# Mixture of experts behind cross-attention: first tiles of experts 4 to 7 from five items, narrower two-group tiles, and a later load of the last items' inputs

## The chip, the cores and the metric

The kernel runs on one core of a Trainium2 chip. The metric is the device time of one execution in microseconds; the median of the runs of the kernel before is 442.06.

## The reference, cut to what matters

Eight items (batch elements) of 256 tokens with 256 features go through a cross-attention block and then through a feed-forward layer with eight experts, of which each token uses two.

```python
x = x + xattn(layernorm(x), ctx, ctx, mask, gamma, beta)   # ctx: 8 x 77 x 256; softmax over 77; layernorm of the result
h = layernorm(x)                                           # 2048 tokens
p = softmax(h @ w_gate)                                    # 8 experts; keep the two largest, divide by their sum
gu = einsum('bsd,edh->ebsh', h, w_gate_up)                 # per expert 256 x 2048
act = silu(g) * u                                          # g, u: the halves of gu, 1024 each
x = x + sum over experts of p_e * (act_e @ w_down_e)       # per expert 1024 x 256
```

The kernel computes an expert only for the tokens that chose it. There are 4096 token-expert pairs.

## The kernel before, in words

**The two kinds of work.** A *unit* (`unit(b)`, L445) is one item: its attention, its normalised row, its choice of two experts, and the place of each token in the list of its expert. It ends with two stores: the item's x to the output (L826, SyncE's queue) and its normalised rows with gate values to a scratch tensor `xn_rows` (L860, ScalarE's queue; item 1's on SyncE's). A *tile* (`tile_work(t)`, L1214) takes rows of one expert: GpSimd gathers them from `xn_rows` (L1195) by a list of indices; TensorE transposes them (L1278); ScalarE copies them (L1285); TensorE forms g and u (L1335), ScalarE silu (L1357), VectorE the product (L1364), TensorE the down product (L1396, or L1393 in turned form); VectorE multiplies by the gate (L1445), and GpSimd adds the rows to the output by a scattering DMA (L1199). VectorE computes the gate of a tile (L1292) from the gathered rows.

**The tiles.** Tiles 0 to 7 are the *first tiles* of experts 0 to 7, up to 128 rows each. They can start before all items are routed: `PARTS` says after how many items which experts' first tiles are filled, `(2, 0, 1)`: expert 0 after two items, `(3, 1, E)`: experts 1 to 7 after three. For each entry `first_table(i)` (L922) takes the lists as they stand: a product on TensorE picks the tokens (L934), VectorE writes the indices (L947) and clears those experts in the lists (L951), a second product gives the counts (L938), and an expert with fewer than 128 tokens begins to count anew (L957 to L966). The counting of the next item waits for that. After item 7, `second_table` (L976) divides what is left into tiles: thirteen *narrow* tiles of 128 rows, and eight *wide* ones of two groups, one per expert, of 128 rows and of `WIDE[k]` rows. The experts are sorted by their remainder, and the k-th gets the k-th width. Where a remainder exceeds its width, it takes another narrow tile; more than thirteen of those would go through a slow path (`rest_tile`). A wide tile costs its whole width W = 128 + `WIDE[k]`, filled or not; with `WIDE[k]` below 100 the down product is turned, so that it too costs W columns. `ORDER1` sets the order of narrow and wide tiles.

**The order.** Every operation is recorded by `add(engine, cost, emit, needs, rank, lag, ...)`; `Order.run` then simulates the engines with these costs and lags and writes out an order for each engine, where among operations that can begin at nearly the same time the lowest rank goes first. On the chip each engine follows its order and waits for what an instruction needs. Units rank before tiles on TensorE, so the units' pieces stand between the tiles' groups of eight matmuls. Matmuls on constant data (`fill`, L327) keep TensorE busy until tile 0 begins.

**The loads.** Expert weights are 1 MB each for the two halves of gate-up (L264) and for down (L265); three sets of buffers (lanes) hold them, tile t of the first eight using lane t mod 3. SyncE issues them in the planner's order. At the start the inputs of items 0 to 5 (`UE = UA + 3`, `UA` the number of items of the last entry of `PARTS`, 3) and the weights of tile 0 and gate-up of tile 1 are issued. What is left, `load_late` (L257), has the down matrix of tile 1 and x and mask of items 6 and 7; it waits for one-element memsets on VectorE (L1313 to L1315) that need tile 0's gate, which holds it back until item 1's store and tile 0's gather are through. Tile 2's weights are held back in the same way until the gate of tile 1.

Of the kernel before, what the change touches and what calls it, by code (L numbers as in the profile page):

```python
# [33 lines left out]
class Order:  # L34
# [18 lines left out]
    def add(self, eng, cost, emit=None, needs=(), rank=0.0, lag=None, takes=(), uses=(), after=(), slack=0.0):  # L53
        lag = self.LAG[eng] if lag is None else lag
        w = Work(eng, cost, emit, list(needs), list(after), rank, lag, list(takes), slack)
        for b in list(takes) + list(uses):
            b.users.append(w)
        self.all.append(w)
        return w
# [61 lines left out]
def kernel(  # L121
# [36 lines left out]
    nc = tc.nc  # L158
    P = 128
    B, S, D = x.shape  # L160
    T = ctx_in.shape[1]
    E = w_gate.shape[1]
# [7 lines left out]
    NL = N // P  # L170
    LANES = 3

    PARTS = [(2, 0, 1), (3, 1, E)]
    UF, UA = PARTS[0][0], PARTS[-1][0]
    UE = UA + 3
    MT0 = E

    WIDE = [128, 120, 104, 96, 80, 64, 48, 24]
    assert len(WIDE) == E and E * NL == P


# [54 lines left out]
    wd = [keep.tile([P, NF, D], F32, name=f"wd{l}") for l in range(LANES)]  # L236

    def load(what, dst, src, b0, b1, per):
        what.dma_start(dst[:, b0 * per : b1 * per, :], src[:, b0 * per : b1 * per, :])
# [14 lines left out]
    load(nc.sync, x_all, x_t, UA, UE, NT)  # L254
    load(nc.sync, m_all, mask_t, UA, UE, NT)

    def load_late():  # L257
        nc.sync.dma_start(wd[1], w_down[1].rearrange("(c p) d -> p c d", p=P))
        load(nc.sync, x_all, x_t, UE, B, NT)
        load(nc.sync, m_all, mask_t, UE, B, NT)  # L260

    def weight_dmas(l, gu, d, **kw):
        for up in range(2):
            nc.sync.dma_start(wgu[l][:, :, ts(up, F)], gu[:, :, ts(up, F)], **kw)  # L264
        nc.sync.dma_start(wd[l], d, **kw)  # L265

    def load_expert(l, e):
        weight_dmas(
            l,
            w_gate_up[e].rearrange("(c p) f -> p c f", p=P),  # L270
            w_down[e].rearrange("(c p) d -> p c d", p=P),
        )
# [23 lines left out]
    def iota(dst, pattern, base, mult):  # L296
        nc.gpsimd.iota(
            dst, pattern=pattern, base=base, channel_multiplier=mult, allow_small_or_imprecise_dtypes=True
        )
# [31 lines left out]
    add = order.add  # L331
# [19 lines left out]


    c_in = [add("in", 0.0, lag=3.8 if b == 0 else 7.3 if b < UA else 14.0) for b in range(B)]
    late = add("sp", 1.0, load_late, [], -1999.0, lag=5.0)
    x_in = [add("in", 0.0, lag=(4.2, 7.0, 10.0)[b] if b < UA else 17.0) if b < UE else late for b in range(B)]
    m_in_ = [add("in", 0.0, lag=4.3 if b == 0 else 11.6 if b < UA else 18.6) if b < UE else late for b in range(B)]
    wg_in = add("in", 0.0, lag=4.6)
# [78 lines left out]

    anew = [const.tile([P, E], BF16, name=f"anew{i}") for i in range(len(PARTS))]
    ahead = list(before)
    for i, (units, _, _) in enumerate(PARTS):
        ahead[units * NT] = anew[i]  # L440
# [460 lines left out]
    def table_constants():  # L901
# [12 lines left out]
        for k in range(E):  # L914
            nc.gpsimd.memset(widths[:, k : k + 1], float(WIDE[k]))
        iota(bases, [[NL, E]], 0, 0)
# [5 lines left out]
    def first_table(i):  # L922

        units, e0, e1 = PARTS[i]
        last = routed[units - 1]
# [237 lines left out]

    snaps = [first_table(i) for i in range(len(PARTS))]
    table = [None, second_table([p[1] for p in snaps])]


    def weights_of(at, m):
        e = nc.sync.value_load(at[0:1, m : m + 1], min_val=0, max_val=E - 1)
        return (  # L1170
            w_gate_up[bass.ds(e, 1)].rearrange("o (c p) f -> p (o c) f", p=P),
            w_down[bass.ds(e, 1)].rearrange("o (c p) d -> p (o c) d", p=P),
        )

    def load_weights(t):
        f, m, l = tiles[t]
        if f == 0:
            return load_expert(l, m)
        kw = {}
        if f == 1:  # L1180
            kw = dict(cond=nc.sync.value_load(new[0:1, m : m + 1], min_val=0, max_val=1), cond_hint=False)
        weight_dmas(l, *weights_of(eid_w if f == 2 else eid, m), **kw)

    def part_of(t):
        return next(i for i, (_, e0, e1) in enumerate(PARTS) if e0 <= tiles[t][1] < e1)

# [24 lines left out]
    def known(w):  # L1211
        return [] if w is None else [w]

    def tile_work(t):  # L1214
# [4 lines left out]
        if wide:  # L1219
            n = WIDE[m]  # L1220
            groups = [(P, idx[1][:, MT1 + m : MT1 + m + 1]), (n, idx[1][:n, MT1 + E + m : MT1 + E + m + 1])]
# [11 lines left out]
        r, rp = -1000.0 + t, 1.0e6 + 100.0 * t  # L1233
# [7 lines left out]
        if t < LANES - 1:  # L1241
            weights = add("in", 0.0, lag=(24.0, 33.0)[t])
        elif f == 0:
            needs += [w for s in stored[:UF] for w in s] if t < LANES else []
            if t == LANES - 1:

                needs.append(
                    add("dve", 0.08, lambda: nc.vector.memset(wgu[l][:1, 0, :1], 0.0), [held_back["gc"]], r)
                )
            weights = add("sp", 2.0, lambda: load_weights(t), needs, r, lag=8.0)  # L1250
        else:
            weights = add("sp", 1.0, lambda: load_weights(t), needs, r, lag=8.0 if wide else 3.0)

        b_x, got, where = [], [], []
        for n, at in groups:
# [3 lines left out]
            def gather(n=n, at=at, dst=where[-1]):  # L1259
                pool_rows(t, at, dst[:n], in_=xn_d)  # L1260
                if t == MB - 1:
# [5 lines left out]
                    lag=3.0, takes=[b_x[-1]], after=gathers[-1:],  # L1267
# [19 lines left out]
        def gate(i):  # L1287
            n, src = groups[i][0], where[i]
            gs = hpool.tile([P, 2], F32, tag="gs", name=f"gs{t}_{i}", bufs=4)
            v["gc", i] = hpool.tile([P, 1], F32, tag="gc", name=f"gc{t}_{i}", bufs=4)  # L1290
            mine = float(m) if f == 0 else em_w[:n, m : m + 1] if wide else em[:n, L1 + m : L1 + m + 1]
            nc.vector.scalar_tensor_tensor(  # L1292
                gs[:n], src[:n, EXP : EXP + 2], mine, src[:n, GATE : GATE + 2],
                ALU.is_equal, ALU.mult, accum_out=v["gc", i][:n],
            )
# [5 lines left out]
        if t == 0:  # L1301
            held_back["ex"].after.append(xT)
            add("pe", 0.0, lambda: fills.update(stop=True), [tp], rp - 129, lag=0.0)
        gc = [
            add("dve", 0.25, lambda i=i: gate(i), [got[i]] + known(et), r, takes=[b_gs[i]], uses=[b_x[i]])
            for i in range(len(groups))
        ]


        if t == 0:  # L1310

            late.needs += [
                add("dve", 0.08, lambda: nc.vector.memset(wd[1][:1, 0, :1], 0.0), gc, r),  # L1313
                add("dve", 0.08, lambda: nc.vector.memset(x_all[:1, UE * NT, :1], 0.0), gc, r),
                add("dve", 0.08, lambda: nc.vector.memset(m_all[:1, UE * NT, :1], 0), gc, r),  # L1315
            ]
# [206 lines left out]
    for t in range(MB):  # L1523
        if t == MT0:
            guessed = add(
                "sp", 3.0, lambda: load_expert(TURN1[0], HELD[0]), [lane_last[TURN1[0]]], -1000, lag=3.0
            )
        tile_work(t)
# [40 lines left out]
```

## Time and profile before

| | |
|---|---|
| median of three runs | 442.06 us (441.53 to 445.3) |
| profiled execution | 441.23 us, span 439.5 us |
| TensorE busy | 426.5 us (97%) |
| VectorE, ScalarE, GpSimd busy | 151.8, 121.7, 132.2 us |
| two thirds of TensorE's time | g and u, 268.0 us in 1856 matmuls |
| down products | 127.0 us in 592 matmuls |
| read and written by DMA | 102.69 MB and 8.71 MB |

How to read the rows: a line of a timeline has the start, the length, the engine, the line of the kernel, the operation, output and inputs by the program's names, shapes and the number of instructions; in brackets stands the idle time ahead of it and what ended it. A matmul's row lasts longer than its turn, since matmuls overlap: eight g of 128 columns follow one another in 0.89 us though each row lasts 0.28. A row of windows has the window, its length, the busy times of TensorE, its weight loads, VectorE, ScalarE and GpSimd with instruction counts, the granted clock of TensorE, the share of the DMA engines and GB/s.

### The profile page before, as it was taken

What the parts mean: (1) busy time and instruction counts of PE and PEld (TensorE: products, weight loads), DVE (VectorE), ACT (ScalarE), POOL (GpSimd) and SP (SyncE); (2) the same over time, 40 slices, a digit from 0 to 9 for tenths busy, and PEclk for the clock granted to TensorE, in tenths of its full rate; (3) what the DMA queues carried; (4) which work ended last, traced back from release to release, by engine and by line L of the source; (5) the groups of instructions that cost most, each with busy time, mean ns of one, the idle gap of its engine ahead of it and who ended that gap; (6) DMA issues with size and microseconds to landing.
All of it is one profiled execution on the core that took longest, in us unless ns stands there. A gap on an engine that the chain in (4) does not pass through costs nothing. (4 is left out here: it accounts for less than half of the span.)

```text
span 439.5 us, 8064 instructions
## 1 busy us (share of the span) xinstructions
PE 426.5 (97%) x2961; PEld 398.8 (91%) x2961; DVE 151.8 (35%) x682; ACT 121.7 (28%) x298; POOL 132.2 (30%) x155
## 2 busy tenths in 40 slices
PE   8998899999999999999999999999999999999995
PEld 6877789899999998999999999999999999999994
DVE  4897268766772122111111221112121112212111
ACT  6785466863311111011111111111111111221110
POOL 7642552432216230332033202321413304212121
PEclk9999889999999999999999999999999999999999
DMA  6995598999998994883289945376428257781011
GB/s 157 335 354 151 170 388 260 328 303 316 322 322 255 383 326 110 283 269 81 88 239 304 319 168 157 95 248 209 115 41 297 32 188 228 230 279 17 9 18 34
DMA packets 54563, 92.58 MB, mean 211 GB/s; under 512 B 5544, under 2 KB 41124, under 8 KB 54513
## 3 DMA queue, kind: packets, MB, share of 16 engines
q1 hardware_dynamic: 45388, 81.25, 54.7%
q0 software_dynamic: 6688, 8.59, 10.2%
q10 hardware_dynamic: 2437, 2.11, 1.5%
q8 instruction: 26, 0.43, 0.4%
q14 instruction: 24, 0.20, 0.1%
HBM read 102.69 MB, written 8.71 MB: 253 GB/s over the span
## 5 line engine op out<-in xcount | busy, mean ns | idle before, releaser
L1335 PE MATMUL g<-xgT,wgu 128*128 128x128 f32 (+8 forms) x928 | 134.1, 294 | 0.5 <-ACT xgT L1285 0.5
L1335 PE MATMUL u<-xgT,wgu 128*128 128x128 f32 (+8 forms) x928 | 133.9, 294 | 0.0
L1335 PEld LDWEIGHTS g<-xgT,wgu 128*128 128x128 f32 x928 | 123.1, 191 | 2.4 <-ACT xgT L1285 0.7
L1335 PEld LDWEIGHTS u<-xgT,wgu 128*128 128x128 f32 x928 | 123.4, 191 | 1.6
L1364 DVE TENSOR_TENSOR hT<-sil,u 128x512 f32<-128x512 f32 (+7 forms) x74 | 47.9, 648 | 167.2 <-PE u L1335 162.2
L1199 POOL DMA_INDIRECT out_dram<-y,idx x37 | 57.5, 1554 | 148.5 <-DVE gs L1292 78.3
L1396 PE MATMUL o<-wd,hT 128*128 128x256 f32 (+2 forms) x432 | 100.4, 385 | 0.0
L1396 PEld LDWEIGHTS o<-wd,hT 128*128 128x128 f32 (+2 forms) x432 | 81.1, 193 | 10.9
L1357 ACT ACTIVATE sil<-g 128x512 f32<-128x512 f32 (+7 forms) x74 | 41.8, 565 | 149.4 <-PE g L1335 143.1
L1195 POOL DMA_INDIRECT xg<-xn_rows,idx x37 | 39.0, 1055 | 109.1 <-PE tp L1278 88.0
L1285 ACT COPY xgT<-tp 128x256 f32<-128x256 f32 (+8 forms) x29 | 11.9, 411 | 102.9 <-PE tp L1278 102.5
L1445 DVE TENSOR_SCALAR y<-o,gc 128x256 f32<-128x256 f32 (+2 forms) x26 | 12.6, 484 | 54.0 <-PE o L1396 54.0
L1393 PE MATMUL o<-hT,wd 128*128 128x224 f32 (+4 forms) x160 | 26.6, 324 | 0.0
L1393 PEld LDWEIGHTS o<-hT,wd 128*128 128x128 f32 x160 | 25.9, 190 | 0.0
L327 PE MATMUL filled<-filler 128*128 128x256 bf16 x114 | 17.1, 289 | 1.3 <-DVE cT L396 1.3
L1278 PE MATMUL tp<-ident,xg 128*128 128x128 f32 (+7 forms) x74 | 12.8, 269 | 2.6 <-DMA xg<-xn_rows,idx 2.6
L1278 PEld LDWEIGHTS tp<-ident,xg 128*128 128x128 f32 (+7 forms) x74 | 9.7, 141 | 5.9 <-DMA xg<-xn_rows,idx 3.1
L1445 DVE TENSOR_SCALAR y<-rows,gc 128x256 f32<-128x256 f32 (+5 forms) x10 | 4.3, 476 | 28.4 <-PE rows L1425 28.4
L327 PEld LDWEIGHTS <-filler 128*128 128x128 bf16 x114 | 11.1, 104 | 3.0 <-DVE cT L396 1.3
L833 POOL TENSOR_TENSOR rx<-ss,neg_half 128x2 f32<-128x2 f32 x8 | 5.7, 707 | 19.7 <-DVE ss L830 19.3
L1413 ACT COPY oT<-o 128x224 f32<-128x224 f32 (+4 forms) x10 | 3.2, 318 | 28.2 <-PE o L1393 28.2
L645 PE MATMUL v<-av_w,pT 77*128 77x256 f32 x32 | 9.6, 426 | 0.8 <-ACT xT L522 0.8
(207 smaller groups left out, 306.2 us busy)
## 6 DMA issues: line engine op xcount, KB each, us to landing
wgu<-in_L_ffn_w_gate_up_dram SPq DMA_DIRECT2D x60, 1024.0 KB
wd<-in_L_ffn_w_down_dram SPq DMA_DIRECT2D x30, 1024.0 KB
out_dram<-x_all SPq DMA_DIRECT2D x8, 256.0 KB
xn_rows<-xnr ACTq DMA_DIRECT2D x7, 260.0 KB
x_all<-in_x_dram SPq DMA_DIRECT2D x3, 256.0 KB
x_all<-in_x_dram SPq DMA_DIRECT2D x1, 768.0 KB
xg<-xn_rows,idx POOLq DMA_INDIRECT x37
out_dram<-y,idx POOLq DMA_INDIRECT x37
```

The costliest lines, as they stand in the source:

```text
L327: nc.tensor.matmul(filled, filler[:, :P], filler, start=True, stop=True)
L645: nc.tensor.matmul(v["v"][:, j, :], v["pT"][:, j, :], av_w[:, b, KC:], start=True, stop=True)
L1195: nc.gpsimd.indirect_dma_start(out=tile_, out_offset=None, in_=in_[:n], in_offset=at, bounds_check=n - 1, oob_is_err=False)
L1199: nc.gpsimd.indirect_dma_start(out=out_[:n], out_offset=at, in_=tile_, in_offset=None, bounds_check=n - 1, oob_is_err=False, **kw)
L1278: nc.tensor.transpose(v["tp"][:, c, off : off + n], src[:n, ts(c, P)], ident[:n, :n])
L1285: nc.scalar.copy(v["xT"][:, :, :W], v["tp"][:, :, :W])
L1335: nc.tensor.matmul(v[tag, h][:, i, : W if wide else P], wgu[l][:, c, bass.ds(off + (h + i) * P, P)], v["xT"][:, c, : W if wide else P], st ...
L1357: nc.scalar.activation(v["sil", h], v["g", h][:, :, : min(W, per)], AF.Silu)
L1364: nc.vector.tensor_tensor(v["hT", h // held][:, bass.ds(h % held, FG), : min(W, per)], v["sil", h], v["u", h][:, :, : min(W, per)], ALU.mult,)
L1393: nc.tensor.matmul(v["o", d][:, :W], wd[l][:, i, ts(d, P)], hT[:, :W], **kw)
L1396: nc.tensor.matmul(v["o", d][:n], hT[:, offs[d] : offs[d] + n], wd[l][:, i, :], **kw)
L1445: nc.vector.tensor_scalar(v["y", i][:n], src, gc, None, ALU.mult)
```

## The change

`PARTS` gets a third entry: experts 1 to 3 are filled from three items, experts 4 to 7 from five, so there is a third first table, after item 4, and tiles 4 to 7 gather only after item 4's rows are stored. `UA` stays 3. Five of the eight widths of the wide tiles fall. The late load is split: the down matrix of tile 1 is loaded as before, held by tile 0's gate (`load_down`); x and mask of items 6 and 7 come after tile 2's weights in SyncE's order (`late.after`), held by tile 1's gate, and the planner gets another rank and lag for them.

```diff
-    PARTS = [(2, 0, 1), (3, 1, E)]
-    UF, UA = PARTS[0][0], PARTS[-1][0]
+    PARTS = [(2, 0, 1), (3, 1, 4), (5, 4, E)]
+    UF, UA = PARTS[0][0], PARTS[1][0]
...
-    WIDE = [128, 120, 104, 96, 80, 64, 48, 24]
+    WIDE = [128, 120, 104, 88, 72, 48, 40, 16]
...
+    def load_down():
+        nc.sync.dma_start(wd[1], w_down[1].rearrange("(c p) d -> p c d", p=P))
+
     def load_late():
-        nc.sync.dma_start(wd[1], w_down[1].rearrange("(c p) d -> p c d", p=P))
         load(nc.sync, x_all, x_t, UE, B, NT)
         load(nc.sync, m_all, mask_t, UE, B, NT)
...
-    late = add("sp", 1.0, load_late, [], -1999.0, lag=5.0)
+    late = add("sp", 1.0, load_late, [], -997.9, lag=11.0)
...
             weights = add("sp", 2.0, lambda: load_weights(t), needs, r, lag=8.0)
+            if t == LANES - 1:
+                late.after.append(weights)
...
         if t == 0:
-
+            hold = add("dve", 0.08, lambda: nc.vector.memset(wd[1][:1, 0, :1], 0.0), gc, r)
+            add("sp", 0.5, load_down, [hold], r, lag=3.0)
+        if t == LANES - 2:
             late.needs += [
-                add("dve", 0.08, lambda: nc.vector.memset(wd[1][:1, 0, :1], 0.0), gc, r),
                 add("dve", 0.08, lambda: nc.vector.memset(x_all[:1, UE * NT, :1], 0.0), gc, r),
                 add("dve", 0.08, lambda: nc.vector.memset(m_all[:1, UE * NT, :1], 0), gc, r),
             ]
```

## The prediction

> **What bounds the kernel now.** I read the page first. Its parts 1 and 2:
>
> ```profile
> span 439.5 us, 8064 instructions
> PE 426.5 (97%) x2961; PEld 398.8 (91%) x2961; DVE 151.8 (35%) x682; ACT 121.7 (28%) x298; POOL 132.2 (30%) x155
> PE   8998899999999999999999999999999999999995
> PEclk9999889999999999999999999999999999999999
> ```
>
> TensorE is the bound: from 60 us to its last matmul it is full, except for 0.85 us near 81. So a change counts only if it shortens TensorE's stream, or opens or closes a hole in it. The holes lie before 60 us, and there the clock row shows an 8 twice. So the next view is TensorE's timeline there:
>
> ```profile
> 48.01 1.02 PE L528 MATMUL lps<-cT,xT 128*128 128x86 f32 x8
> 50.52 0.44 PE L1278 MATMUL tp<-ident,xg 128*128 128x128 f32 x2 [1.49 <-DMA xg<-xn_rows,idx]
> 50.79 1.03 PE L1396 MATMUL o<-wd,hT 128*128 128x256 f32 x4
> 52.44 1.12 PE L640 MATMUL gkp<-av_w,pT 77*128 77x85 f32 x4 [0.62 <-DVE xw L605]
> 53.36 1.98 PE L645 MATMUL v<-av_w,pT 77*128 77x256 f32 x4
> 55.13 4.60 PE L1396 MATMUL o<-wd,hT 128*128 128x256 f32 x12
> ```
>
> and the same stretch in windows of 2 us, where the granted clock (third from the right) halves at 52 us:
>
> ```profile
> 50.00:52.00 2.00, 1.30 (x6) 0.85 (x6) 0.43 (x7) 0.37 (x1) 1.48 (x2) 1.00 0.36 83
> 52.00:54.00 2.00, 1.56 (x6) 1.50 (x7) 0.56 (x3) 1.20 (x4) 1.86 (x3) 0.51 0.78 246
> 58.00:60.00 2.00, 2.00 (x10) 1.66 (x10) 1.68 (x13) 1.40 (x6) 0.48 (x1) 0.78 1.04 377
> ```
>
> Tile 1's gathered rows come 1.49 us late. Who held them: GpSimd's timeline, ScalarE's queue, and the DMA queues from 44 to 46 us (q10 is ScalarE's, q1 SyncE's; packets, MB, share).
>
> ```profile
> 40.41 0.40 ACTq L860 DMA_DIRECT2D xn_rows<-xnr  x1
> 47.52 1.09 POOL L1195 DMA_INDIRECT xg<-xn_rows,idx  x1 [9.59 <-DMA xn_rows<-xnr]
> ...
> q1 hardware_dynamic: 380, 0.32, 98.6%
> q10 hardware_dynamic: 36, 0.04, 11.2%
> ...
> q10 hardware_dynamic: 222, 0.22, 63.0%
> q1 hardware_dynamic: 354, 0.12, 46.3%
> ```
>
> Item 2's rows, issued at 40.4 to 40.8, move only from 44.5 to 46.1, and the gather starts 1.4 us later. In front stand the three transfers of the late load: one 1.05 MB down matrix, 0.52 MB of x, 0.16 MB of mask.
>
> **The change, part by part.** *Narrower tiles.* The cost is read from whole tiles: W=224 takes 287.27 to 305.43 (18.16 us), W=208 takes 317.24 to 334.12 (16.88), W=176 takes 14.32, W=152 takes 12.40. The slope is 0.080 us a column. The five changed widths lose 8+8+16+8+8 = 48 columns: -3.84 us, all on TensorE and hidden by nothing. All five were below the limit of 100 for the turned product, so the form stays. The routing of the given inputs fits: after five items every expert holds at least 128 rows, the sorted remainders are 114, 90, 73, 45, 19, 18, 15, 10, nothing spills and 13 narrow tiles suffice. With the old split the remainders 89, 73 would spill.
>
> *The late load.* The down matrix stays where it was; x and mask of items 6 and 7 go behind tile 2's weights on SyncE's queue. Item 2's store then has 0.68 MB less ahead, at 0.35 MB/us 1.9 us. The gather starts near 45.6 and lands 3.0 us later (47.52 to 50.5), 48.6, against 49.0 when TensorE gets there: the hole falls from 1.49 to about 0.2, -1.3. In the new order v of item 3 precedes gkp; gkp still waits for the xw of item 4, which stands behind tile 3's gate on VectorE: 0.62 becomes 0.5, -0.1. The half clock has cost gkp 0.55 (1.12 against 0.57 at full clock), v 0.87 (1.98 against 1.11), the twelve o 1.84 (4.60 against 0.385+11x0.216): 3.3 us. It goes if the hole goes.
>
> Here two rules of the Trainium skill speak against the rows. "TensorE: Matmul & The Clock Gate", section "HAM oscillation — how this bites in real kernels", warns of idle gaps above about 3.4 us. By that the holes of 1.49 and 0.62 could not have halved the clock, its return would not be ours to win, and a new hole of 1 to 3 us would be free of it. By the row they did halve it, while 1.13 and 0.46 around 38 us did not; I follow the row, so 3.3 us are won here and can be lost at any new hole of 1.5 us or more. "DMA: Bandwidth & Descriptors", section "Queues, rings and completion order", lets each engine alternate between the queues at packet boundaries. Then SyncE's transfers would not hold ScalarE's store, and the move would win nothing of these 4.7 us. The row shows 3.7 us before the first byte of q10; I follow it, and keep the other as a rival.
>
> Also queued behind the moved load: tile 3's weights start 0.68/0.37 = 1.8 us later; first used near 85 and landed near 72, they have 12 us of cover. Items 6 and 7 get x near 63 (from 51.5: 3.15 MB, then 0.68, then the landing), needed near 68. On GpSimd the mask operation of item 6 now precedes ry of item 4: 0 to 1 us on that chain. The three 0.06 us memsets are only split: nothing.
>
> *A third first table.* TensorE: ids and n_e, 0.29 and 0.17 by the rows of table two, with fills +0.4. VectorE: idx 0.17, lists 0.28, taken 0.16, stays 0.07 and 0.17, anew 0.17: 1.0 us in a stage where it is 70 to 90% busy. It hides unless VectorE is late for the list product.
>
> *Tiles 4 to 7 wait for item 4.* Their gathers were issued between 51 and 80 us with tens of us to spare. Now four stand in a row on GpSimd behind item 4's store, before ry of item 5 and tile 2's scatter. When does TensorE ask? Tile 1's first product moves from 59.79 to 59.79-1.3-0.1-3.3 = 55.1. From there to tile 4's transposes before needed 31.1 us (to 90.91); less item 7's logits 0.86, item 6's pps 0.22, a rank 0.1 and half of the 0.85 wait, plus 0.4: 29.9, so 85.0. When are the rows there? Item 4's gkp begins at 55.1+6x0.89+0.75 = 61.2; before, its store was issued 11.0 later (69.56 to 80.60): 72.2. Stores under load took 5.1 to 5.4 to the last byte (items 2, 3, 4), plus 1.4: 78.9. Gather: 1.1 to issue, then 1.9 if the queues are idle (tile 9) or 5.0 if loaded (tile 3: issued by 51.2, its gate ran at 56.25). So 81.9 to 85.0. Zero to 0.2 by the rows, but the chain has no slack left; I take 1.2. The lower end is 0, the upper 5.1 (second rival). VectorE's gates of tiles 5 and 6 may hold it as the gate of tile 3 did:
>
> ```profile
> 56.25 0.16 DVE L1292 SCALAR_TENSOR_TENSOR gs<-xg 128x2 f32<-128x2 f32 x1 [3.69 <-DMA xg<-xn_rows,idx]
> ```
>
> That delays item 5's chain, whose ranks TensorE reaches 6.6 us after tile 4: covered up to about 3 us.
>
> *The second table comes later.* Items 6 and 7 end later among the tiles. Its list product moves from between tile 6's gate-up groups to between its down groups; tile 8's transposes, before 7.2 us after it (131.29 to 138.54), now follow two down groups and three of tile 7, 4.7 us later. The gather starts 1.35 after the product, plus 1.05 and 1.9 to 5.0: 4.3 to 7.4. A hole of 0 to 2.7; tile 9's weights are issued just then, so 1.5.
>
> *The 0.85 us near 81* (item 5's v behind ScalarE's copy for item 7): the order there is new, 0 to -0.85; I take -0.4.
>
> **Sum.** The profiled execution took 441.23, 1.7 outside its span. -3.84 -1.3 -0.1 -3.3 +0.4 +1.2 +1.5 -0.4 = -5.84: 435.4. The median of the runs, 442.06, lies 0.8 above the profiled run, the lowest 0.3; I add 0.6: 436.0.
>
> **Rivals.** *A: a new hole halves the clock.* As the forecast, with 3.3 given back at tile 4 or 8: 439.3. For it: 1.5 us sufficed at 50 us. Against: the estimated holes are that size only together. *B: the first hole stays*, the queues taking turns as the skill says: only -0.5 of the 4.7, nothing at tile 4 (TensorE comes 4 us later): 441.23-3.84-0.5+0.4-0.4+1.5 = 438.4, with 0.6: 439. *C: slower.* Item 4's store goes strictly behind what SyncE has queued. That queue ran full from 51.5 to 72.5 for 7.4 MB; 0.7 MB more and 0.4 less end near 73, then item 4's output and tile 4's 3.15 MB at 0.37 end near 82, the store 0.7 later, the gather at 83.8, its rows with 1.1+5.0 at 89.9: a hole of 5.1 (3.9 more than taken), the clock with it (3.3), and once more at tile 8 (3.3): 446.5. It turns slower than before when tile 4's rows land after about 89 with one clock loss. Against it: the three stores measured took 5.1 to 5.4 whatever stood ahead. *D: no new hole at all*: 433.3. That the narrower tiles spill into the slow rest path is excluded by the counts.
>
> **How the numbers follow.** Forecast 0.36 (434 to 438), A 0.22, B 0.16, C 0.18, D 0.08. About 1% (4.4 us) is what a measurement of this kernel tells from no change: faster means below 437.6, slower above 446.5. Faster: nearly all of the forecast, D, a part of A and B, 0.49. Slower: over half of C with some slip, 0.13. Same: 0.38. The range takes A and B whole and most of C: 433.5 to 445.5.
>
> **What would show it.** Right: tile 1's first gather near 45.6, clock 1.0 from 50 to 60, tile 1's groups from 55; tile 4's transposes near 86 with a wait of 0 to 2 on its rows; tile 8's near 137; a W=144 tile of 11.8 us. Wrong: a gather of tile 1 still near 47.5, or a clock of 0.5 near 85 or 137.

## The result, and the profile after

The changed kernel takes 449.16 us, the median of four runs (446.96 to 450.25), against 441.79 for the kernel before on the same chip: a ratio of 1.0162 with a 95% interval of 1.0127 to 1.0197. It is slower by about 7 us where 6 us less were forecast, and lies outside the range given. The profiled execution took 450.25 us, 9.0 more than that of before.

The page of the kernel after, its span, TensorE's totals and two rows of 40 slices (busy share and granted clock, in tenths):

```profile
span 448.5 us, 8075 instructions
PE 428.3 (95%) x2964; PEld 401.2 (89%) x2964; DVE 151.0 (34%) x690; ACT 121.2 (27%) x298; POOL 132.7 (30%) x155
...
PE   8999999689999889999999999999999999999993
...
PEclk9999999959999999999999999999999999999997
```

A slice has 11.2 us. The two 8s of before in the clock's row, near 50 us, are gone. In their place one slice, from 89.7 to 100.9 us, has a clock of 5 tenths, the one ahead of it has TensorE busy for 6 tenths only, and two more 8s in TensorE's row stand from 146 to 168. A *hole*, from here on, is time in which TensorE stands idle. To place the loss, both traces are cut at the first g of a tile:

| stretch of TensorE | before | after | difference |
|---|---|---|---|
| start to tile 1's first g | 59.79 | 55.95 | -3.84 |
| tile 1 to tile 2 | 16.36 | 15.75 | -0.61 |
| tile 2 to tile 3 | 14.98 | 18.68 | +3.70 |
| tile 3 to tile 4 | 14.09 | 20.11 | +6.02 |
| tile 4 to tile 8 | 44.58 | 49.88 | +5.30 |
| tile 8 to the last down product | 280.68 | 276.79 | -3.89 |
| from there to the end of the span | 9.02 | 11.34 | +2.32 |

The first stretch answers to the lines shown of before. TensorE's timeline of the kernel after:

```profile
49.65 0.44 PE L1282 MATMUL tp<-ident,xg 128*128 128x128 f32 x2
...
52.62 0.65 PE L642 MATMUL gkp<-av_w,pT 77*128 77x85 f32 x4 [0.81 <-DVE xw L607]
...
55.95 1.95 PE L1341 MATMUL g<-xgT,wgu 128*128 128x128 f32 x16
```

No wait ahead of tile 1's transposes any more, 0.65 instead of 1.12 us for gkp: the late load's move does what was forecast of it. Thirty microseconds on, the same view:

```profile
85.23 1.06 PE L647 MATMUL v<-av_w,pT 77*128 77x256 f32 x4
89.90 0.69 PE L1282 MATMUL tp<-ident,xg 128*128 128x128 f32 x2 [3.61 <-DMA xg<-xn_rows,idx]
90.38 3.62 PE L1341 MATMUL g<-xgT,wgu 128*128 128x128 f32 x16
95.39 1.98 PE L530 MATMUL lps<-cT,xT 128*128 128x86 f32 x8 [1.39 <-DVE v L694]
97.16 1.98 PE L1341 MATMUL u<-xgT,wgu 128*128 128x128 f32 x8
```

In the kernel before, the logits of item 7 (`lps`) and the transposes of tile 4 had no wait in front of them:

```profile
83.42 1.07 PE L528 MATMUL lps<-cT,xT 128*128 128x86 f32 x8
...
90.91 0.38 PE L1278 MATMUL tp<-ident,xg 128*128 128x128 f32 x2
```

In the kernel after, the transposes at 89.90 are tile 4's; the g behind them is tile 3's, whose rows were transposed at 71.48. TensorE stands in front of tile 4's rows with tile 3's work ready, because its order has tile 4's transposes first. Then 16 products that take 1.95 us elsewhere take 3.62. Windows of 1 us show why (the third column from the right is the granted clock):

```profile
88.00:89.00 1.00, 0.00 (x0) 0.00 (x0) 0.00 (x0) 0.00 (x0) 0.97 (x2) 0.67 1.01 379
...
101.00:102.00 1.00, 1.00 (x7) 1.00 (x6) 0.62 (x2) 0.11 (x2) 0.00 (x0) 0.50 0.00 0
102.00:103.00 1.00, 1.00 (x11) 1.00 (x11) 0.76 (x5) 0.00 (x0) 0.69 (x1) 1.00 0.00 0
```

Half the clock from 88.3 (0.67 over the microsecond) to 102.0. Of that, 89.9 to 102.0 less the 1.39 of the second hole is 10.7 us of work, which lost half: 5.35 us. Holes and clock together, 3.61 + 1.39 + 5.35 = 10.35, less the hole of 0.85 near 81 that is gone, are within 0.3 us of the 9.72 that the stretches from tile 2 to tile 4 lost. About 2 of the 5.35 lie ahead of the logits at 95.39, whose start another engine sets (below); the clock's own cost is the 3.3 behind them. Of the 5.30 after tile 4, 2.83 are holes (below); most of the rest, 1.7 us, is pieces of items 6 and 7 that stood ahead of tile 4 before.

Why the rows were late. ScalarE's queue and GpSimd's timeline, kernel after:

```profile
73.96 0.37 ACTq L862 DMA_DIRECT2D xn_rows<-xnr  x1
```

```profile
83.21 1.16 POOL L1197 DMA_INDIRECT xg<-xn_rows,idx  x1 [5.54 <-DVE x_all L544]
...
87.30 1.00 POOL L1197 DMA_INDIRECT xg<-xn_rows,idx  x1 [0.30 <-issue]
88.32 0.73 POOL L586 TENSOR_TENSOR rq<-ss,neg_half 128x2 f32<-128x2 f32 x1
92.44 1.64 POOL L1201 DMA_INDIRECT out_dram<-y,idx  x1 [3.39 <-DVE y L1451]
93.57 1.28 POOL L674 TENSOR_TENSOR ry<-vy,neg_half 128x2 f32<-128x2 f32 x1
```

Item 4's store is issued at 73.96, and the gather of tile 4 starts 9.25 us later. The releaser named there, a VectorE operation that ended at 82.8, is not what it waited for in the program; the store's last bytes fit. The DMA queues of the kernel after in 78 to 80, 80 to 82 and 82 to 84 us (packets, MB, share; q1 is SyncE's, q10 ScalarE's):

```profile
q1 hardware_dynamic: 120, 0.48, 62.7%
...
q10 hardware_dynamic: 117, 0.12, 17.3%
...
q10 hardware_dynamic: 136, 0.13, 18.2%
...
q10 hardware_dynamic: 1, 0.00, 0.0%
```

q10 moves its first packets between 76 and 78 (18 of them) and its last at 82.0: 8.0 us from the issue. SyncE had issued tile 4's three weight transfers, 3.15 MB, at 69.8 to 72.1, just ahead.

Two more places. VectorE, kernel after, in front of the second hole:

```profile
89.88 0.16 DVE L1296 SCALAR_TENSOR_TENSOR gs<-xg 128x2 f32<-128x2 f32 x1 [7.09 <-DMA xg<-xn_rows,idx]
...
91.59 0.16 DVE L1296 SCALAR_TENSOR_TENSOR gs<-xg 128x2 f32<-128x2 f32 x1 [1.54 <-DMA xg<-xn_rows,idx]
...
92.19 0.16 DVE L1296 SCALAR_TENSOR_TENSOR gs<-xg 128x2 f32<-128x2 f32 x1
...
92.27 0.23 DVE L664 SCALAR_TENSOR_TENSOR junk<-gkp,prob 128x77 f32<-128x77 f32 x1
```

VectorE waits for the rows of tiles 4, 5 and 6 in turn to compute their gates. Behind them stand the square sums of item 5 (L664), whose gkp was ready at 85.4. From these come vy, ry on GpSimd (93.57), the gate logits, and with them the release of the one buffer in PSUM (where TensorE's products land) of item 5's gkp, which the logits product of item 7 waits for. And near 156 us, VectorE again, followed by TensorE's row:

```profile
156.87 0.22 DVE L1296 SCALAR_TENSOR_TENSOR gs<-xg,em_w 128x2 f32<-128x2 f32 x1 [3.39 <-DMA xg<-xn_rows,idx]
...
157.36 0.69 DVE L1370 TENSOR_TENSOR hT<-sil,u 128x512 f32<-128x512 f32 x1 [0.26 <-issue]
```

```profile
158.10 1.99 PE L1402 MATMUL o<-wd,hT 128*128 128x256 f32 x8 [2.58 <-DVE hT L1370]
```

The gates of tile 9, a wide one, wait for rows that were gathered late, since the second table comes later; tile 7's last product of silu(g) and u stands behind them, and TensorE's down products behind that.

### The profile page after: what moved, and what is told of

It is laid out like the page before. It is cut to its first block, busy times and chain, and to the rows that moved or that the text cites. A ratio compares the mean times of both kernels' runs of the same rounds, so it can differ in the third digit from the quotient of the medians.

```text
span 448.5 us, 8075 instructions
## 1 busy us (share of the span) xinstructions
PE 428.3 (95%) x2964; PEld 401.2 (89%) x2964; DVE 151.0 (34%) x690; ACT 121.2 (27%) x298; POOL 132.7 (30%) x155
## 5 line engine op out<-in xcount | busy, mean ns | idle before, releaser
L1402 PE MATMUL o<-wd,hT 128*128 128x256 f32 (+2 forms) x432 | 99.1, 381 | 2.8 <-DVE hT L1370 2.8
L1370 DVE TENSOR_TENSOR hT<-sil,u 128x512 f32<-128x512 f32 (+7 forms) x74 | 47.4, 641 | 157.7 <-PE u L1341 156.5
L1402 PEld LDWEIGHTS o<-wd,hT 128*128 128x128 f32 (+2 forms) x432 | 79.4, 189 | 13.4 <-DVE hT L1370 3.4
L1289 ACT COPY xgT<-tp 128x256 f32<-128x256 f32 (+8 forms) x29 | 11.8, 407 | 100.7 <-PE tp L1282 100.2
L1399 PE MATMUL o<-hT,wd 128*128 128x216 f32 (+4 forms) x160 | 25.3, 317 | 0.0
L1399 PEld LDWEIGHTS o<-hT,wd 128*128 128x128 f32 x160 | 24.7, 190 | 0.0
L530 PE MATMUL lps<-cT,xT 128*128 128x86 f32 x64 | 10.2, 312 | 2.4 <-DVE v L694 2.4
L530 PEld LDWEIGHTS lps<-cT,xT 128*128 128x128 f32 x64 | 9.5, 227 | 3.3 <-issue 1.7
L580 ACT ACTIVATE sq_x<-x_all,nm 128x256 f32<-128x256 f32 x16 | 8.1, 506 | 14.4 <-DVE nm L827 11.3
```

The costliest lines, as they stand in the source:

```text
L530: nc.tensor.matmul(v["lps"][:, j, :], v["xT"][:, c, j, :], cT[:, b, c, :CT], start=(c == 0), stop=(c == NC - 1))
L1289: nc.scalar.copy(v["xT"][:, :, :W], v["tp"][:, :, :W])
L1370: nc.vector.tensor_tensor(v["hT", h // held][:, bass.ds(h % held, FG), : min(W, per)], v["sil", h], v["u", h][:, :, : min(W, per)], ALU.mult,)
L1399: nc.tensor.matmul(v["o", d][:, :W], wd[l][:, i, ts(d, P)], hT[:, :W], **kw)
L1402: nc.tensor.matmul(v["o", d][:n], hT[:, offs[d] : offs[d] + n], wd[l][:, i, :], **kw)
```

## The experiments

**The late load alone.** The kernel after with two lines put back:

```diff
-    PARTS = [(2, 0, 1), (3, 1, 4), (5, 4, E)]
+    PARTS = [(2, 0, 1), (3, 1, E)]
-    WIDE = [128, 120, 104, 88, 72, 48, 40, 16]
+    WIDE = [128, 120, 104, 96, 80, 64, 48, 24]
```

> The kernel after with the old PARTS and the old WIDE, so only the late load is moved. My theory now: the move does what it was forecast to do at the first hole (tile 1's groups at 55.95 instead of 59.79 in the profile after), and the loss of the kernel after comes from tiles 4 to 7 waiting for item 4. Then tile 1's first g comes near 56, the clock stays 1.0 from 50 to 60, a hole of about 1 us near 67 stays (GpSimd's mask operation of item 6 waits for its mask ahead of item 4's ry), and the whole takes 441.8 - 3.8 + 1 = 438 to 440. Rival: the late inputs of items 6 and 7 are what delays the later items; then this kernel is slower than before as well, 444 or more.

Measured: 438.71 us against 441.97 (ratio 0.9925, 0.9902 to 0.9948). Tile 1's first g comes at 54.76, the clock is 1.0 over the whole execution. One hole is left after tile 1, in TensorE's timeline:

```profile
67.31 1.09 PE L530 MATMUL lps<-cT,xT 128*128 128x86 f32 x8 [2.00 <-DVE v L694]
```

The move is a gain of 3.3 us by itself: in the traces 5.0 at tile 1, of which the new hole gives 2.0 back.

**The split and the widths alone.** The kernel before with the other three lines changed (PARTS, WIDE, and UA, which stays 3).

> The kernel before with the new PARTS and the new WIDE, the late load where it was. My theory: the first hole and its half clock come back (tile 1's first g near 59.8), so TensorE asks for tile 4's rows some 3.8 us later than in the kernel after (86.3 + 3.8 = 90.1), while item 4's store has a queue shorter by 0.68 MB: rows near 89 to 91, a hole of 0 to 1 us at tile 4 and no half clock there; 3.9 us fewer for the widths, 1 to 3 us more for VectorE's gates that wait for rows: 439 to 443. Rival: the third first table and the changed order of items 5 to 7 cost by themselves, whatever the late load does: 448 or more, with a hole of 3 us or more at tile 4.

Measured: 448.15 us (442.79 to 451.24; ratio 1.0162, 1.0093 to 1.0230). The rival's number held. The trace is that of the shortest of its four runs, 442.79, 1.6 above the trace of before; what the other three lost beyond it, no trace shows. Even there tile 4's transposes wait:

```profile
91.43 0.44 PE L1278 MATMUL tp<-ident,xg 128*128 128x128 f32 x2 [2.73 <-DMA xg<-xn_rows,idx]
```

Item 4's store is issued at 76.03 there, 2.1 us later than in the kernel after, and the gather starts at 84.32, 1.1 later. I had expected the smaller queue and TensorE's later arrival to close the hole; they close 0.9 of 3.61. The first hole, which I had expected back, is not there either: tile 1's transposes run at 51.81 without a wait, because TensorE was held up before, by a hole of 1.54 us at tile 0 and half the clock from 38.5 to 45.3, and tile 1's first g comes at 57.02, 1.1 us behind the kernel after. By the medians the split costs by itself, and the late load's gain is not added to it: the kernel after is as slow as this one. The traces fit this: from 88.7 here to 86.3 in the kernel after TensorE asks for tile 4's rows 2.4 us earlier, but the rows come only 1.5 earlier.

**Tile 4's transposes later in TensorE's order.**

```diff
-        tp = add("pe", 0.25 * len(groups), turn, got, rp - 130, takes=[b_tp], uses=b_x)
+        tp = add("pe", 0.25 * len(groups), turn, got, rp - (82 if f == 0 and t == 4 else 130), takes=[b_tp], uses=b_x)
```

> The kernel after with tile 4's transposes put behind tile 3's g and u in TensorE's order, instead of ahead of them; nothing else is asked for. If the place of the transposes is the whole cause, the 3.61 us at 86 to 90 and the half clock after it go: 449.2 - 3.6 - 5.3 = 440. My theory: a second wait stands right behind. VectorE's gates of tiles 5 and 6 wait for the same gathers until 92.2, item 5's square sums, ry and gate logits stand behind them, and the logits product of item 7 waits for their buffer until about 95.2; TensorE reaches it two groups after 86.3, at 88.3, and stands there some 7 us. Then the gain is about nothing, 447 to 450.

Measured: 450.45 us (448.79 to 450.7; ratio 1.0178, 1.0118 to 1.0237). As the theory had it, the hole moves to item 7's logits and grows; TensorE's timeline:

```profile
95.27 1.98 PE L530 MATMUL lps<-cT,xT 128*128 128x86 f32 x8 [6.60 <-DVE v L694]
```

95.27 against 95.39 in the kernel after. The waits stand behind one another, and the later one sets the end.

**The gates behind their tile's transposes.**

```diff
-            add("dve", 0.25, lambda i=i: gate(i), [got[i]] + known(et), r, takes=[b_gs[i]], uses=[b_x[i]])
+            add("dve", 0.25, lambda i=i: gate(i), [got[i], *([xT] if t >= 4 else [])] + known(et), r, takes=[b_gs[i]], uses=[b_x[i]])
```

> The kernel after with each gate on VectorE from tile 4 on placed behind its tile's own copy of the transposed rows, so that no gate stands ahead of item 5's chain or of tile 7's product while its rows are under way; tile 4's transposes stay where they are. My theory: the hole of 3.6 us at tile 4 stays and halves the clock as before, the hole of 1.4 us in front of item 7's logits goes, and the 2.6 us at 155.5 to 158.1 (tile 7's product behind the gates of tile 9) go: 449.2 - 1.4 - 2.6 = 445. Rival: those holes wait for the weights or for the transposes and not for the gates: 449, holes unchanged.

Measured: 443.14 us (ratio to before 1.0038, 1.0014 to 1.0062), 6 us less than the kernel after, where 4 were expected. TensorE's timeline:

```profile
89.54 0.44 PE L1282 MATMUL tp<-ident,xg 128*128 128x128 f32 x2 [3.61 <-DMA xg<-xn_rows,idx]
...
92.44 1.82 PE L530 MATMUL lps<-cT,xT 128*128 128x86 f32 x8
```

The first hole is untouched, the second gone, and the hole at 156 has become 2.0 at tile 8's transposes. The expectation left out the clock: it is half only from 90.7 to 94.1 here, a quarter of the time that it was half in the kernel after.

**Both edits.**

> The kernel after with both edits at once: tile 4's transposes behind tile 3's g and u, and each gate from tile 4 on behind its tile's transposes. Alone, the first gave nothing (450.5, the wait moved to item 7's logits) and the second took 6 us (443.1, the hole of 3.6 us and half a clock of 5 us left). My theory: the two waits cover each other, and with both gone the hole at 86 to 90, the logits' hole and the half clock are gone together: 443.1 - 3.6 - 2.4 = 437, more than the two gains added. Rival: a third wait stands behind (the gather's rows for tile 5, item 5's chain): 441 or more.

Measured: 445.24 us (ratio 1.0081, 1.0055 to 1.0106): a miss, and by the medians slower than the gates alone, though the two intervals touch. TensorE's row at item 7's logits is

```profile
92.53 1.98 PE L530 MATMUL lps<-cT,xT 128*128 128x86 f32 x8 [4.09 <-DVE v L694]
```

with no gate ahead of item 5's square sums on VectorE (they run at 85.8, vy is done at 86.4). The third wait is in GpSimd's timeline:

```profile
87.64 1.00 POOL L1197 DMA_INDIRECT xg<-xn_rows,idx  x1 [0.30 <-issue]
88.66 0.73 POOL L586 TENSOR_TENSOR rq<-ss,neg_half 128x2 f32<-128x2 f32 x1
89.58 1.64 POOL L1201 DMA_INDIRECT out_dram<-y,idx  x1 [0.19 <-issue]
90.70 1.28 POOL L674 TENSOR_TENSOR ry<-vy,neg_half 128x2 f32<-128x2 f32 x1
```

ry of item 5, 1.28 us of work, stands behind four gathers that wait for item 4's store until 83.5 and take 1.0 to 1.2 us each with 0.3 between, behind rq of item 7 and a scatter. The same late rows hold three engines: TensorE by the transposes, VectorE by the gates, GpSimd by the gathers themselves, and item 5's chain passes through two of them. With one hole of 4.09 instead of 3.61, the clock is half for 6.8 us (92.3 to 99.1) instead of 3.4: 0.5 + 1.7 us, of the 2.7 by which this trace is the longer.

**Tile 4's weights held back until item 4's store.**

```diff
+            if t == 4:
+                needs += [add("dve", 0.08, lambda: nc.vector.memset(wgu[l][:1, 0, :1], 0.0), stored[4][1:], r)]
             weights = add("sp", 2.0, lambda: load_weights(t), needs, r, lag=8.0)
```

> The kernel after with tile 4's weights (3.15 MB) issued only after item 4's store of rows, by one more memset on VectorE; TensorE's order and the gates are as in the kernel after. My theory: the 8.0 us from the store's issue (73.96) to its last byte (82.0) are the queue in front of it. With that load behind it the store takes 3 to 5 us, the gather starts at 77 to 79 in place of 83.2, tile 4's rows land at 81 to 85, ahead of TensorE (86.3): no hole, no half clock, no wait of the logits; the 2.6 us near 156 stay: 449.2 - 3.6 - 1.4 - 5.3 = 439. Rival: the store is slow by itself or for the gather's own sake; then the gather stays near 83 and the time at 447 to 450.

Measured: 447.1 us (445.07 to 449.73; ratio 1.0110, 1.0081 to 1.0139), some 2 us less where 10 were expected; the trace is that of the longest run. In its parts the mechanism is confirmed: the store, issued at 75.11, moves its last bytes at 78.2 (272 of its packets from 75 to 79, none after), 3.1 us instead of 8.0; tile 4's transposes at 87.28 have no wait. Yet the gather starts only at 81.37, 1.8 us earlier than in the kernel after, for now its list is last, which VectorE writes at 80.93; GpSimd's row:

```profile
81.37 1.16 POOL L1197 DMA_INDIRECT xg<-xn_rows,idx  x1 [2.55 <-DVE idx L949]
```

And the gates wait on: those of tiles 5 and 6 for rows that come at 89.3 and 91.6, VectorE's rows:

```profile
91.58 0.16 DVE L1298 SCALAR_TENSOR_TENSOR gs<-xg 128x2 f32<-128x2 f32 x1 [1.74 <-DMA xg<-xn_rows,idx]
...
91.67 0.23 DVE L664 SCALAR_TENSOR_TENSOR junk<-gkp,prob 128x77 f32<-128x77 f32 x1
```

so item 7's logits wait 4.16 us and the clock is half from 92.6 to 99.4, and once more behind a hole of 2.76 near 156. The expectation's "no wait of the logits" forgot that four gathers land one after the other.

**The holes filled.** The waits stay; 36 products on constant data are put ahead of tile 4's transposes and 28 ahead of item 7's logits:

```diff
+                    if t == 4 and c == 0:
+                        for _ in range(36):
+                            nc.tensor.matmul(v["tp"].rearrange("p c k -> p (c k)"), filler[:, :P], filler, start=True, stop=True)
                     nc.tensor.transpose(v["tp"][:, c, off : off + n], src[:n, ts(c, P)], ident[:n, :n])
...
             if b == 7:
+                early["u"] = psum([P, 4, P], "c", "u3_0")
+                for _ in range(28):
+                    nc.tensor.matmul(
+                        early["u"][:, :2, :].rearrange("p i k -> p (i k)"), filler[:, :P], filler, start=True, stop=True
+                    )
```

> The kernel after with products on constant data, 36 ahead of tile 4's transposes and 28 ahead of item 7's logits (0.107 us each), which fill the two holes with work that nobody needs; no wait is removed and no order changed. My theory: the holes are still waited out, but the clock stays at 1.0 from 88 to 102, and what follows 95.4 runs at full speed: 3.3 us less, 446. Rival: the half clock costs nothing there, since the work behind it waits for VectorE and ScalarE anyway, or the clock falls for another reason: 449, clock 0.5 as before.

Measured: 449.28 us (445.73 to 450.48; ratio 1.0130, 1.0075 to 1.0184), no gain that can be told as a whole. The stage says otherwise. TensorE's timeline:

```profile
87.79 4.09 PE L1291 MATMUL tp<-filler 128*128 128x256 bf16 x36
91.72 0.38 PE L1292 MATMUL tp<-ident,xg 128*128 128x128 f32 x2
...
93.72 3.22 PE L531 MATMUL u<-filler 128*128 128x256 bf16 x28
97.00 1.09 PE L537 MATMUL lps<-cT,xT 128*128 128x86 f32 x8
...
108.72 0.39 PE L1292 MATMUL tp<-ident,xg 128*128 128x128 f32 x2
```

From item 7's logits to the next tile's transposes it takes 11.7 us (97.00 to 108.72) against 14.9 in the kernel after (95.39 to 110.26), at a clock of 1.0: 3.2 us less, of 3.3 expected. So the half clock is a cost of its own, and the idle time sets it. In this execution two things outside the stage hide it: tile 0's transposes waited 2.46 us for their rows, with the half clock behind them, and tile 1 began 1.6 later; and the hole near 156, 2.46 us here, halved the clock from 157.7 to 161.1, which 2.58 us in the kernel after had not done. Four runs spread over 4.7 us can't show 3 us.

**The planner told what the profile shows.**

```diff
-            lag=3.5, uses=[b_row],
+            lag=8.0 if b == 4 else 3.5, uses=[b_row],
...
-                    lag=3.0, takes=[b_x[-1]], after=gathers[-1:],
+                    lag=5.6 if t >= 4 else 3.0, takes=[b_x[-1]], after=gathers[-1:],
```

with the gates behind the transposes as above.

> The kernel after, its planner told what the profile shows: a gather from tile 4 on lands 5.6 us after it is issued instead of 3.0, item 4's store is through after 8.0 instead of 3.5, and a gate waits for its tile's transposes. The planner then puts tile 4's transposes behind three pieces of tile 3's g and u and item 7's logits. My theory: no hole of over 1 us behind 68 us, no half clock: 437 as with both edits, or lower by up to 2 since tile 8's transposes come later too (2.0 us of hole at 149 with the gates alone): 435 to 437. Rival: holes move elsewhere: 441 or more.

Measured: 440.75 us (ratio 0.9955, 0.9931 to 0.9979): at the rival's edge. One hole is left in the stage, 2.73 us at item 7's logits (91.09), with the half clock from 91.5 to 94.9. GpSimd again: ry of item 5 at 89.82, behind three gathers, a scatter and a gather, where vy was there at 85.2.

**The gathers apart.** The last, and

```diff
-                    "pool", 1.05, gather, known(ix) + [s[1] for s in units], r,
+                    "pool", 1.05, gather, known(ix) + [s[1] for s in units] + (turned_[-1:] if 4 < t < MT0 else []), r,
```

where `turned_` holds the transposes of the tiles so far.

> The kernel with the measured lags and the late gates (440.75), and one edit more: in the planner the gathers of tiles 5, 6 and 7 wait for the transposes of the tile before, so that only tile 4's stands ahead of item 5's ry on GpSimd. My theory: what was left there, 2.73 us of TensorE at 88.4 to 91.1 and 3.6 us of half clock behind it, is GpSimd's queue, in which vy of item 5 (ready at 85.2) waits until 89.8 behind three gathers, a scatter and a fourth gather. With one gather and the scatter ahead, ry begins at 87 to 88 and the logits of item 7 come without a hole of over 1 us: 440.75 - 2.2 - 1.8 = 436.5 (436 to 438). Rival: ry is held by something else, or tile 5's rows are now late at their turn: 440 to 442.

Measured: 438.1 us (436.7 to 438.7; ratio 0.9920, 0.9900 to 0.9940), at the upper edge of what was expected. GpSimd's timeline:

```profile
83.34 1.16 POOL L1198 DMA_INDIRECT xg<-xn_rows,idx  x1 [0.17 <-DMA wd<-in_L_ffn_w_down_dram]
85.61 1.59 POOL L1202 DMA_INDIRECT out_dram<-y,idx  x1 [1.11 <-DVE y L1453]
86.68 1.28 POOL L675 TENSOR_TENSOR ry<-vy,neg_half 128x2 f32<-128x2 f32 x1
88.15 1.13 POOL L1198 DMA_INDIRECT xg<-xn_rows,idx  x1 [0.18 <-PE pps L634]
```

Tile 4's gather is no earlier than in the kernel after (83.34 against 83.21), its rows are no earlier either (transposes at 90.08), and TensorE waits 0.48 us for them and 0.38 for item 7's logits; the clock stays up. The late rows cost under 1 us here, where what doesn't need them is not queued behind them. But this kernel is only level with the late load alone (0.9920 against 0.9925), though its widths save 3.84 us. Between the two traces, the stretch from tile 2's transposes to tile 9's takes 1.6 us more here (92.1 against 90.6), and the end of the span 2.2 more (see the end of the next section).

**The mask operation later on GpSimd.** One more number in the planner:

```diff
-    late = add("sp", 1.0, load_late, [], -997.9, lag=11.0)
+    late = add("sp", 1.0, load_late, [], -997.9, lag=14.0)
```

> As the last, and the planner is told that the late inputs land 14 us after their issue instead of 11, which puts the mask operation of item 6 on GpSimd behind ry of item 4. The hole of 1.0 us at 65.6 to 66.7 (logits of item 6, behind the gate logits of item 4, behind ry, behind the mask operation that waited 4.7 us for its mask) should go: 1 us less than the last. Rival: the mask is needed right behind it and item 6 waits instead: no difference.

Measured: 436.6 us (435.06 to 439.8; ratio 0.9897, 0.9867 to 0.9927). The mask operation now follows ry of item 4 (64.70), and the wait of 1.24 us at 67.3 in the last kernel is gone. (It stood ahead of item 5's logits, which need the buffer of item 4's gkp; the expectation calls them item 6's.) The two intervals overlap, so the gain is not shown; the profiled runs are 1.0 us apart.

**Narrower still.** With the gathers apart, and the widths close to the remainders of this routing:

```diff
-    WIDE = [128, 120, 104, 88, 72, 48, 40, 16]
+    WIDE = [120, 96, 80, 56, 32, 24, 24, 16]
```

> As the one with the gathers apart, with WIDE fitted closer to the sorted remainders of this routing (114, 90, 73, 45, 19, 18, 15, 10): 120, 96, 80, 56, 32, 24, 24, 16 instead of 128, 120, 104, 88, 72, 48, 40, 16. 168 columns less in all. At the 0.080 us a column of the forecast, 13.4 us, if the two widest stay in the same form of the down product; the second (96) is below 100 and turned now, 128 + 96 = 224 columns, which took 18.16 us as a whole tile in the kernel before: 436.5 - 13.4 = 423. Rival: a narrower tile leaves less time for the next tile's weights (3.15 MB a tile at 0.37 MB/us is 8.5 us, a tile of 144 columns takes 11.8), and a second bound, the loads, takes part of it: 426 or more.

Measured: 423.48 us (421.97 to 426.06; ratio 0.9612, 0.9583 to 0.9640), faster than before by almost 4% and than the kernel after by more. The loads take no part of it: after tile 0 no hole is over 1.1 us. These widths suit this routing: they leave 6 to 13 rows above each remainder, and another routing may need more than thirteen narrow tiles, that is the slow path. So this is not a gain of the change alone.

And the same for the two first tables, the late load alone with `WIDE = [120, 112, 96, 96, 80, 24, 24, 16]`:

> The kernel with the late load alone moved (old PARTS, two first tables; 438.71), with WIDE fitted as closely to its own sorted remainders (114, 105, 90, 89, 73, 18, 15, 10): 120, 112, 96, 96, 80, 24, 24, 16. It asks what the third first table is worth once nothing waits for it. My theory: a column is worth 0.080 us where the tile is turned and less where it is not; 64 to 24, 48 to 24, 24 to 16 give 72 columns or 5.8 us, 104 to 96 turns the product (232 columns to 224 and 32 products of 256 to 224, about 1.3), the two widest 0.9: 438.7 - 8 = 431, some 7 us behind the kernel with three first tables and narrow widths (423.48), which is the difference of the sums of the widths. Rival: the third table and its waits still cost part of it, and this one comes within 3 us of 423.5.

Measured: 430.56 us (429.9 to 431.96; ratio 0.9762, 0.9731 to 0.9793), 7.1 behind, so the rival is out. Narrow widths alone, without a third first table, gain 7 to 8 us on the late load alone (0.9925, 438.71 us). The third table adds about 7 by the 120 columns that it allows beyond that, once its waits are taken away; the change as made cut 48 columns and paid for them on three engines. Part of the 7 may be the late gates, the lags and the gathers apart, which this kernel has not: a wait of 1.94 us at item 5's logits is left in it. The two tables with those edits were not run.

## Why the prediction was wrong

The forecast's sum was 435.4 for the profiled execution, the measured 450.25: 14.8 us apart. Step by step:

**Narrower tiles**, -3.84: right. The stretch from tile 8 to the last down product is 3.89 shorter, a tile of 144 columns takes 11.76 us (407.00 to 418.76; 11.8 given).

**The late load**, -4.7 at tile 1: right in mechanism, 0.9 short. The gather started at 46.74, not 45.6, and tile 0 itself began 0.76 later in this execution; gkp's wait grew from 0.62 to 0.81 instead of falling to 0.5; the first hole and the half clock behind it are gone. By rival B, with the queues taking turns, it would have stayed, so the forecast did well to follow the row here.

**"Tiles 4 to 7 wait for item 4", taken at 1.2 of 0 to 5.1**: this is the step that failed first. TensorE asked at 86.3 (85.0 given). The store was issued by 74.33 (72.2 given; the prediction counts from the end of the issuing instruction). It took 8.9 from there to the gather where "stores under load took 5.1 to 5.4 to the last byte, plus 1.4" gave 6.7, and the gather 6.67 to its rows where 3.0 to 6.1 was given. Each term was short, all on the same side: rows at 89.88, not 81.9 to 85.0. Three stores were taken as the rule, "whatever stood ahead". Their likeness fits what stood ahead of them, which was much the same: from issue to last byte SyncE's queue moved 1.5, 1.6 and 1.4 MB beside the stores of items 2, 3 and 4 in the kernel before. In that same trace the store of item 0, with 2.5 MB moved beside it, took 7.2 us, and that of item 5, with 1.9, took 6.6; the sample left both out. In the kernel after it was 2.5 MB again, and 7.6 us. For item 4's store in the kernel before, ScalarE's queue has

```profile
80.23 0.37 ACTq L860 DMA_DIRECT2D xn_rows<-xnr  x1
```

and its bytes moved from 83.9 to 86.1, when all but 0.6 of the 3.15 MB issued from 74.3 had moved. In the kernel after the same weights, issued from 69.8, still had tile 3's ahead of them. Rival C counted bytes and had the gather at 83.8 and the rows at 89.9; the trace has 83.21 and 89.88. The run with those weights held back shows that they were what stood ahead (3.1 us for the store instead of 8.0). C's total of 446.5 is right in part by luck: it had a second loss of clock at tile 8, 3.3 us, that did not come, and nothing for the logits or the end. C was given 0.18, and what spoke against it in the prediction was that sample.

**"That delays item 5's chain, whose ranks TensorE reaches 6.6 us after tile 4: covered up to about 3 us"**: the step that failed second, and the one that makes the loss hard to remove. The wrong waiter was named. Not item 5's ranks but the logits of item 7 come first, two groups behind tile 4's transposes, since they need the PSUM buffer of item 5's gkp. The prediction saw that gates of tiles 5 and 6 would stand ahead on VectorE and four gathers ahead of ry on GpSimd, and gave both a price of nothing. It cost 1.39 us in the kernel after, as the hole ahead of the logits. With the transposes moved, that wait alone is 6.60 us; with transposes and gates moved, GpSimd's queue alone is 4.09.

**The clock.** The prediction had the price (a hole of 1.5 us or more can halve it) and put it in the rivals, 3.3 us, but not in the forecast. Work lost 5.35 to it, as the second hole fell into the first one's recovery; the part behind the logits, 3.3 us, is what filling the holes gave back (3.2).

**"Queued behind the moved load ... 0 to 1 us on that chain"** for the mask operation on GpSimd: 0.98 us ahead of item 5's logits, within what was given, but left out of the sum.

**The second table, 1.5 of 0 to 2.7**: 1.3 short (0.25 and 2.58), and wrong in place. Tile 8's transposes at 148.43 had no wait; tile 7's product stood behind tile 9's gates on VectorE.

**The 0.85 near 81**: gone, 0.4 more than taken.

**The end.** From the last down product to the end of the span the kernel after takes 2.3 us more, and the prediction had no term for it. The last scatter starts 4.4 us after the last down products in both, but the span ends 6.9 us after that start instead of 4.6. Seven of the fourteen kernels have 4.6 to 5.4 there (before, both with the late load alone, the narrow one), seven have 6.6 to 7.1, with no edit that divides them. With one trace of each it can't be told from a difference between executions; what sets it was not tried and stays open.

Taken together: 0.9 at tile 1, 2.4 more at tile 4's rows, 1.4 at item 7's logits, 5.35 of clock, 1.0 at the mask, 1.3 at tile 9's gates, 2.3 at the end, 0.45 back at 81: 14.2 of the 14.8. The 2.3 at the end are in this sum without a cause.

## What to carry to other kernels

When a change makes a transfer's data later, list every instruction that waits for them on every engine, transposes, small vector operations and the transfers' own issues alike, and for each what is queued behind it and who asks for that first; the waits run side by side, so taking one away may show nothing while the next one stands (450.45 us with the transposes moved). Size a store's time by the bytes that the queues hold at its issue, not by earlier stores, unless these had as much ahead of them. A list scheduler that believes a load to land in 3 us puts its users 3 us behind it: put the loaded latency of the trace (6.7 us from a gather's start to its rows here, 8.0 for the store) into its numbers first, and only then judge what a change is worth.

## What the runs showed of the hardware

**The clock gate.** In all fourteen traces the granted clock is full or half, and it changes only on a raster. It was half for 3.41 us (late gates), 6.83 (before, both edits) or 13.65 (after), that is 1, 2 and 4 steps of 3.413 us. It had been full ahead of that for 85.33, 47.79, 78.51 and 75.09 us, that is 25, 14, 23 and 22 steps. Where the raster lies differs between executions: it has an edge at 52.04 in the trace of before and at 88.34 in that of after. What decides at an edge is how long TensorE was idle in the step that ends there (the step's length less TensorE's busy time in that window):

| kernel, step (us) | TensorE idle | clock behind it |
|---|---|---|
| late gates, 87.26 to 90.68 | 2.28 | half |
| filled, 154.28 to 157.70 | 2.21 | half |
| after, 84.92 to 88.34 | 2.05 | half |
| before, 48.62 to 52.04 | 1.71 | half |
| late gates, 145.29 to 148.70 | 1.87 | full |
| both edits, 150.30 to 153.71 | 1.53 | full |
| after, 156.60 to 160.02 | 1.50 | full |
| after, 153.19 to 156.60 | 1.32 | full |

Over all traces, from 18 us on, each of the 18 steps at full clock with 2.0 us idle or more was followed by half the clock, and none of the 19 with 1.0 to 1.6; of six in between, three were. The clock came back behind the first step without idle time to speak of (0.01 us at most); a step with 0.2 did not bring it back (after, 95.17 to 98.58). So a hole of 2 to 3 us may or may not cost the clock by where the raster cuts it: 2.46 us near 156 in the filled kernel lay almost in one step, 2.58 there in the kernel after were cut in two. The Trainium skill ("TensorE: Matmul & The Clock Gate", section "HAM oscillation — how this bites in real kernels") gives gaps over about 3.4 us as the bound. By that the falls of before (holes of 1.49 and 0.62 us), of the filled kernel (2.46) and of the planner's numbers (2.73) would not have come; here 2.05 us of a step, in one hole or two, was enough.

**The queues.** Item 4's rows on ScalarE's queue needed 8.0 us behind 3.15 MB on SyncE's and 3.1 without them. It was not strictly one after the other: from 78 to 82 us q10 moved 0.25 MB while q1 moved 1.13. So the store started late (77.6) and was slowed, but ended before q1 was empty; q1 had tile 5's weights from 77.4 on, too.
